# Loads and scaling of an output weight placed at marks within two steps of an attention loop

## The chip, the cores and the metric

The kernel runs on one core of a Trainium2 chip. The metric is device time in microseconds of the whole program, the median of three runs. A separate execution was recorded by the hardware profiler; every time from a "timeline" or a "group" comes from that execution and counts from the start of its span. The engines are PE (TensorE), DVE (VectorE), ACT (ScalarE), POOL (GpSimd) and SP (SyncE, which only issues transfers). Each takes its own instructions in its own order, and instructions of different engines wait for each other by semaphores.

## What is computed

One block of a transformer with modulated layer norms, in float32, 2048 tokens of width 512:

```python
mod = (silu(c) @ wmod).reshape(1, 6, 1, -1)
sa, ca, ga, sb, cb, gb = (mod[:, i] for i in range(6))
ga = (2 * (ga >= 0) - 1) * maximum(abs(ga), 0.25)      # gb likewise
h = layernorm(x) * (1 + ca) + sa
x = x + ga * attention(h, Q_w, ..., O_w, O_b)          # 16 heads of 128, causal
h = layernorm(x) * (1 + cb) + sb
x = x + gb * moe(h)                                    # 64 experts, top 4, and 2 shared ones
```

`attention` ends in a product of the heads' results with O_w (16 x 128 x 512). The kernel multiplies O_w by the gate ga once, so that the product is already gated.

## The kernel before

**Attention.** A loop runs over 80 steps: 16 heads, five steps each (`steps`, `BATCHES`). A step covers one or two pairs of query tiles of 128 rows: pair 7 in step 0, 6 in step 1, 5 and 0, 4 and 1, 3 and 2 in the others. For step n the loop emits, mixed with each other:
- the scores and exponentials of step n+2 (`softmax_work`): PE matmul ps (L408), DVE maximum (L420, L421), ACT exponential (L427), and DVE's normalisation of a finished row tile (L386 to L397);
- for step n+1, the turning of its probabilities: SP moves 32-row blocks of p to pt in 16 transfers (`swap_blocks`, L451, issued at the end of step n-1), and DVE turns each half (L461);
- for step n, the product with the values (`weighted_values`): PE matmul po (L479), ACT's copy of a finished pair to a tile `at` (L488, two buffers), and POOL's store of it to the array `atd` in DRAM (L489);
- a list of fillers for PE. For the last head these are the late rows of the modulation (`late_mod`, L529) and the output product of the first four token tiles over heads 0 to 14 (`begin_output`, L563), one tile in each of steps 1 to 4.

**What sets the order.** `merge` writes out the order by hand. It takes streams of (cost in PE columns, function), always emits from the stream that is furthest behind, and calls each function of `marks` once the given share of the step's whole cost has been emitted. The framework keeps this order on each engine and adds the semaphores. Marks at 0.55 and 0.8 turn the two halves of step n+1.

**The last head before the change.** At the head of its step 0 (L625 to L640) the kernel makes ga from its row (`gate`, DVE L105 to L110), issues from POOL's queue four transfers of 256 KB for the modulation row of cb (L521, `load_mod(4)`), then four of 1 MB that load O_w into the tile `wo` (L631; the profile calls it hT, whose memory it takes over), four of 256 KB for gb (`load_mod(5)`), and then multiplies the 16 heads of `wo` by ga, one POOL instruction of 128 x 512 for each (L636). Only then come, in POOL's order, the stores of the last head's pairs.

Readers of `wo` are `begin_output` (tile t=0, heads 0 to 14, in step 1) and, after the attention loop, the output phase (L899, L915). DRAM's `atd` of head 15 is read near the end of the loop (L658, L659) and in the output phase.

**After attention** come the output product, the second norm, routing, the experts with the shared experts in the gaps, and the gathering of the results. The change does not touch them.

Of the kernel before, what the change touches and what calls it, by code (L numbers as in the profile page):

```python
# [23 lines left out]
def adaln_block_kernel(  # L24
# [23 lines left out]
    nc = tc.nc  # L48
    _, N, D = x.shape
    H, _, DH = Q_w.shape  # L50
# [24 lines left out]
    ga = const.tile([P, D], F32)  # L75
# [48 lines left out]
    with ExitStack() as att:  # L124
# [57 lines left out]
        def make_q(hd, j):  # L182
            qts[hd, j] = project(0, j, hd, qtp, "qt")
# [4 lines left out]
        with tc.tile_pool(name="pre", bufs=1) as pre, tc.manual_schedule():  # L188
# [4 lines left out]
            for b in range(NB):  # L193
                xb = pre.tile([P, 4, D], F32, name="xb", bufs=NB)
                nc.sync.dma_start(
                    out=xb, in_=x[0, b * 512 : (b + 1) * 512, :].rearrange("(i p) d -> p i d", p=P)
                )
                xs.append(xb)
                if b == 0:
                    wms = {}  # L200
                    for i in (1, 0):
                        wms[i] = pre.tile([P, DC, D], F32, name="wm", bufs=2)
                        nc.sync.dma_start(
                            out=wms[i],
                            in_=wmod[:, i * D : (i + 1) * D].rearrange("(k p) n -> p k n", p=P),
# [116 lines left out]
        def make_v(g, t):  # L322

            if t == 0:
                vts[g] = vp.tile([P, NT, HG * DH], F32, name="v")
            wv, vb = groups[g]
            ps = psA.tile([P, HG * DH], F32, name="pv", tag="mm")
            for k in range(DC):
                nc.tensor.matmul(  # L329
                    out=ps,  # L330
                    lhsT=hT[:, k, t * P : (t + 1) * P],
                    rhs=wv[:, k].rearrange("p i d -> p (i d)"),
                    start=(k == 0),
                    stop=(k == DC - 1),
                )
            nc.vector.tensor_add(vts[g][:, t, :], ps, vb)
# [172 lines left out]
        def load_mod(i, queue):  # L509

            if i == 3:
                mods[i] = [ktp.tile([P, 512], F32, name="kt") for _ in range(DC)]
            elif i in (2, 4):
                both = [vow.tile([P, DC, HG, DH], F32, name="wv") for _ in range(2)]
                both = [w.rearrange("p k i d -> p (k i d)") for w in both]
                mods[i] = [both[k // 2][:, (k % 2) * D : (k % 2 + 1) * D] for k in range(DC)]
            else:
                four = [qkw.tile([P, DC, DH], F32, name=("wq", "wk")[k % 2]) for k in range(DC)]
                mods[i] = [w.rearrange("p k d -> p (k d)") for w in four]
            for k in range(DC):  # L520
                queue.dma_start(  # L521
                    out=mods[i][k], in_=wmod[k * P : (k + 1) * P, i * D : (i + 1) * D]
                )

        def late_mod(i, dst):

            pm = psA.tile([P, D], F32, name="pm", tag="mm")
            for k in range(DC):
                nc.tensor.matmul(  # L529
                    out=pm, lhsT=silc[:, k, :], rhs=mods[i][k], start=(k == 0), stop=(k == DC - 1)  # L530
                )
            if i == 4:
                nc.vector.tensor_scalar_add(dst, pm, 1.0)
            else:
                nc.vector.tensor_copy(dst, pm)
# [19 lines left out]
        def begin_output(t):  # L555
# [4 lines left out]
            def one(hd):  # L560
                if hd == 0:
                    box.append(psA.tile([P, D], F32, name="psb", tag="mm"))
                nc.tensor.matmul(  # L563
                    out=box[0],
                    lhsT=abs_[t // 2][:, hd, (t % 2) * P : (t % 2 + 1) * P],
                    rhs=wo[:, hd, :],
                    start=(hd == 0),
                    stop=(hd == H - 2),
                )
                if hd == H - 2:  # L570
                    if t == 0:
                        nc.vector.tensor_mul(rest[0][:, 1], rest[0][:, 0], ga)
                    nc.vector.tensor_add(parts[t], box[0], xts[t])
                    nc.vector.tensor_add(parts[t], parts[t], rest[0][:, 1])

            return [(512, lambda hd=hd: one(hd)) for hd in range(H - 1)]

        left = []

        def flush():  # L580
# [6 lines left out]
        def softmax_work(n):  # L587
            hd, s = steps[n]
            probs[n] = pp.tile([P, PW], F32, name="p")
            out = []  # L590
            for pr, i in tiles_of(s):
                out += softmax_tile(hd, s, pr, i, probs[n])
            return out

        def swap(n):
            flush()
            turned[n] = swap_blocks(steps[n][1], probs.pop(n))

        def turn(n, half):
            turn_blocks(steps[n][1], turned[n], half)  # L600

        with tc.manual_schedule():
            work = softmax_work(0) + softmax_work(1)
            fill = [(1024, lambda t=t: make_v(0, t)) for t in range(NT)]
            fill += [(2048, lambda j=j: make_q(0, j)) for j in (2, 0, 1)]
            merge([work[:4], fill[:8]], [])
            swap(0)
            merge([work[4:], fill[8:]], [])
            swap(1)
            turn(0, 0)  # L610
            turn(0, 1)
            for n, (hd, s) in enumerate(steps):
                if s == 3:
                    if hd + 2 < H:
                        heads[hd + 2] = load_head(hd + 2)
                    if hd % HG == 1 and hd // HG + 2 < NG:
                        groups[hd // HG + 2] = load_group(hd // HG + 2)
                fill = fillers(hd, s)
                if hd == H - 2 and s == 3:
                    load_mod(2, nc.sync)  # L620
                    load_mod(3, nc.sync)
                if hd == H - 2 and s == 4:
                    load_ab(0)
                    fill.append((2048, lambda: late_mod(2, ga)))
                if hd == H - 1 and s == 0:  # L625
                    mag = qkw.tile([P, DC, DH], F32, name="wq")
                    gate(mag.rearrange("p k d -> p (k d)"), ga)
                    load_mod(4, nc.gpsimd)
                    wo = hTp.tile([P, H, D], F32, name="hT")
                    for i in range(0, H, 4):  # L630
                        nc.gpsimd.dma_start(  # L631
                            out=wo[:, i : i + 4, :], in_=O_w[i : i + 4].rearrange("h p d -> p h d")
                        )
                    load_mod(5, nc.gpsimd)
                    for i in range(H):
                        nc.gpsimd.tensor_mul(wo[:, i, :], wo[:, i, :], ga)  # L636
                    fill += [
                        (2048, lambda i=i, dst=dst: late_mod(i, dst))
                        for i, dst in ((3, sb), (4, cb))
                    ]  # L640
                if hd == H - 1 and s == 1:
                    rest = [vow.tile([P, DC, HG, DH], F32, name="wv") for _ in range(2)]
                    rest = [w.rearrange("p (j k) i d -> p j (k i d)", j=2) for w in rest]
                    nc.sync.dma_start(out=rest[0][:, 0], in_=O_b.partition_broadcast(P))
                    for t in range(NE):
                        load_x_tile(t)
                    fill.append((2048, lambda: late_mod(5, gb)))
                if hd == H - 1 and s == 2:
                    gate(rest[1][:, 0], gb)
                if hd == H - 1 and s >= 1:  # L650
                    if s == 2:
                        place = pp.tile([P, PW], F32, name="p")[:, : (H - 1) * 2 * P]
                        load_ab(1, place.rearrange("p (h t) -> p h t", t=2 * P))
                    if s == 3:
                        load_ab(2)
                    if s == 4:
                        nc.vector.tensor_copy(ga, rest[0][:, 1])
                        nc.sync.dma_start(out=last3, in_=atd[H - 1, :, : (NE - 1) * P])  # L658
                        nc.sync.dma_start(out=ones, in_=atd[H - 1, :, (NE - 1) * P : NE * P])  # L659
                    fill += begin_output(s - 1)  # L660
                streams = [weighted_values(hd, s, turned.pop(n)), fill]
                if n + 2 < len(steps):
                    streams.insert(0, softmax_work(n + 2))
                marks = []
                if n + 1 < len(steps):
                    marks.append((0.55, lambda: turn(n + 1, 0)))
                    marks.append((0.8, lambda: turn(n + 1, 1)))
                merge([st for st in streams if st], marks)
                if n + 2 < len(steps):
                    swap(n + 2)  # L670
# [216 lines left out]
    with tc.manual_schedule():  # L887
# [9 lines left out]
        for t in range(NE):  # L897
            ps = psO.tile([P, D], F32, name="pso", tag="y")
            nc.tensor.matmul(  # L899
                out=ps,  # L900
# [8 lines left out]
        for t in range(NE, NT):  # L909
            pr, i = divmod(t, 2)  # L910
# [3 lines left out]
            for hd in range(H):  # L914
                nc.tensor.matmul(  # L915
                    out=ps,
# [281 lines left out]
```

## Time and profile before

| what | value |
|---|---|
| median of 3 runs | 2533.73 us |
| lowest and highest run | 2530.65 and 2536.56 us |
| profiled execution, its own time | 2545.0 us |
| span of the profile | 2543.2 us |
| mean granted TensorE clock | 0.989 |
| four 1 MB loads of O_w on POOL (L631) | 756 ns each to issue |
| sixteen scales of O_w on POOL (L636) | 1306 ns each, 20.3 us in all |
| 128 stores of head results on POOL (L489) | 613 ns each to issue |

The last three rows are from the groups of instructions by line. A POOL or SP row of a transfer is the time to issue it; the data lands later. In a timeline a row gives start, duration, engine, line, operation, tiles (written <- read), their count, and in brackets the idle time of the engine before it with what ended that.

The stage in question as windows of the span (busy us of each engine, granted clock, share of the DMA engines that was busy):

```profile
1653.60:1680.70 27.10, 14.53 (x51) 8.91 (x49) 17.04 (x30) 4.64 (x12) 18.33 (x21) 0.89 0.98 273
1680.70:1690.30 9.60, 9.58 (x21) 4.90 (x22) 7.51 (x9) 1.97 (x6) 9.60 (x9) 0.79 0.41 128
1690.30:1697.40 7.10, 7.10 (x22) 4.00 (x22) 2.67 (x9) 1.53 (x5) 0.55 (x2) 1.00 0.75 186
1697.40:1724.40 27.00, 27.00 (x81) 14.70 (x79) 17.00 (x32) 2.89 (x8) 0.55 (x1) 1.00 0.47 119
```

The columns after the window are its length, then PE, PE's weight loads, DVE, ACT and POOL (instructions in brackets), the clock, the DMA share, and GB/s.

### The profile page before, as it was taken

How to read it: one execution, taken by the hardware profiler on the slowest of the kernel's cores; microseconds unless marked ns; L12 is line 12 of the kernel's file. 1: busy time of each engine (PE TensorE's matmuls, PEld its weight loads, DVE VectorE, ACT ScalarE, POOL GpSimd, SP SyncE). 2: the span in 40 equal slices, each digit the busy share in tenths (PEclk: the TensorE clock that was granted, in tenths of full speed). 3: DMA queues.
4: the chain of work that ended last, by engine and by line, in shares of the span. 5: the costliest groups of instructions: out<-in, count | busy, mean ns of one | idle time of the engine just before them, and what ended most of it. 6: DMA issues, size and time to landing. Idle time of an engine off the chain costs nothing.

```text
span 2543.2 us, 25501 instructions
## 1 busy us (share of the span) xinstructions
PE 2445.4 (96%) x8297; PEld 1484.3 (58%) x8297; DVE 1431.6 (56%) x2737; ACT 647.1 (25%) x1456; POOL 247.3 (10%) x306
## 2 busy tenths in 40 slices
PE   7999999999999999999999999989999999999989
PEld 4666666666666666666666666545444456566534
DVE  4566666666666666666666666663655522222354
ACT  3233323333232333323333333311111121211100
POOL 0000000000000000000000000040000211111163
PEclk9999999999999999999999999999999999999989
DMA  4234434444444343444444434564521467767564
GB/s 137 60 98 97 115 90 108 112 101 111 98 121 107 93 118 99 96 119 101 109 118 101 109 97 97 161 188 135 203 83 50 124 190 229 226 201 233 168 187 138
DMA packets 225420, 326.21 MB, mean 128 GB/s; under 512 B 32100, under 2 KB 140680, under 8 KB 225288
## 3 DMA queue, kind: packets, MB, share of 16 engines
q1 hardware_dynamic: 197960, 251.16, 38.2%
q0 software_dynamic: 18112, 56.64, 7.0%
q10 hardware_dynamic: 9216, 16.78, 1.7%
q8 instruction: 67, 1.10, 0.2%
q14 instruction: 65, 0.53, 0.1%
HBM read 139.91 MB, written 41.94 MB: 72 GB/s over the span
## 4 chain that ended last, share of the span: by engine, by line
PE 65%; DVE 18%; SPq 6%; issue 4%; DMA 4%; ACT 2%; another core or an unknown queue 1%; DVEq 0%; ACTq 0%; POOL 0%; POOLq 0%
PE pqk L169 12%; PE ps L408 12%; PE po L479 9%; PE psg L973 8%; DVE pt L461 6%; SPq L451 6%; PE pv L329 5%; PE pso L915 4%; PE pse L1064 4%; PE psd L991 4%; DVE nm L421 4%; DMA pt<-p 3%; DVE p L397 3%; PE psy L1083 2%; PE tpx L1057 1%
## 5 line engine op out<-in xcount | busy, mean ns | idle before, releaser
L427 ACT ACTIVATE p<-ps,nm 128x1024 f32<-128x1024 f32 (+7 forms) x384 | 332.2, 865 | 1041.4 <-DVE nm L425 368.5
L408 PE MATMUL ps<-kt,qt 128*128 128x512 f32 (+3 forms) x1280 | 536.6, 536 | 44.5 <-ACT p L427 43.6
L479 PE MATMUL po<-pt,v 128*128 128x256 f32 (+1 forms) x2304 | 568.2, 369 | 6.6 <-DVE pt L461 3.6
L479 PEld LDWEIGHTS po<-pt,v 128*128 128x128 f32 x2304 | 426.2, 191 | 221.7 <-issue 156.5
L421 DVE TENSOR_REDUCE nm<-ps 128x1 f32<-128x1024 f32 (+7 forms) x384 | 349.6, 910 | 92.2 <-PE ps L408 83.4
L461 DVE STREAM_TRANSPOSE pt<-pt 128x1664 f32<-128x1664 f32 (+2 forms) x160 | 318.0, 1988 | 66.3 <-DMA pt<-p 61.5
L408 PEld LDWEIGHTS ps<-kt,qt 128*128 128x128 f32 x1280 | 235.4, 191 | 195.4 <-issue 127.4
L420 DVE TENSOR_TENSOR ps<-ps,causal 128x128 f32<-128x128 f32 x256 | 74.5, 291 | 349.9 <-PE ps L408 349.9
L329 PE MATMUL pv<-wv,hT 128*128 128x256 f32 x1024 | 240.3, 379 | 0.0
L489 POOL DMA_DIRECT2D atd<-at x128 | 78.4, 613 | 1652.2 <-ACT at L488 1627.7
L169 PE MATMUL pqk<-hT,wq 128*128 128x512 f32 x512 | 231.5, 595 | 0.0
L169 PE MATMUL pqk<-hT,wk 128*128 128x512 f32 x512 | 231.2, 595 | 0.0
L397 DVE TENSOR_SCALAR p<-p,rs 128x1024 f32<-128x1024 f32 (+7 forms) x384 | 221.8, 606 | 9.3 <-DMA p<-atd 0.2
L329 PEld LDWEIGHTS pv<-wv,hT 128*128 128x128 f32 x1024 | 194.5, 190 | 31.4 <-issue 1.9
L915 PE MATMUL pso<-hT,v 128*128 128x512 f32 x384 | 175.5, 604 | 0.0
L169 PEld LDWEIGHTS pqk<-hT,wk 128*128 128x128 f32 x512 | 98.0, 192 | 102.3 <-issue 99.7
L169 PEld LDWEIGHTS pqk<-hT,wq 128*128 128x128 f32 x512 | 97.9, 191 | 97.3 <-issue 94.2
L973 PE MATMUL psg<-h2T,wsu 128*128 128x512 f32 x256 | 119.2, 610 | 10.4 <-DVE sig L963 10.4
L1064 PE MATMUL pse<-wgu,xbT 128*128 128x256 f32 x512 | 121.1, 379 | 0.0
L973 PE MATMUL psg<-h2T,wsg 128*128 128x512 f32 x256 | 116.2, 593 | 4.8 <-ACT h2T L750 2.8
L915 PEld LDWEIGHTS pso<-hT,v 128*128 128x128 f32 x384 | 70.7, 192 | 74.5 <-issue 73.7
L991 PE MATMUL psd<-wsd,hs 128*128 128x512 f32 x256 | 111.5, 592 | 0.0
(224 smaller groups left out, 1723.0 us busy)
## 6 DMA issues: line engine op xcount, KB each, us to landing
pt<-p SPq DMA_DIRECT2D x768, 104.0 KB
pt<-p SPq DMA_DIRECT2D x256, 124.0 KB
pt<-p SPq DMA_DIRECT2D x256, 108.0 KB
atd<-at POOLq DMA_DIRECT2D x128, 128.0 KB
wgu<-in_L_ffn_Wg_dram SPq DMA_DIRECT2D x64, 256.0 KB
wgu<-in_L_ffn_Wu_dram SPq DMA_DIRECT2D x64, 256.0 KB
wd<-in_L_ffn_Wd_dram SPq DMA_DIRECT2D x64, 256.0 KB
ybd<-y ACTq DMA_DIRECT2D x64, 256.0 KB
```

Source lines behind the costliest of these rows:

```text
L169: nc.tensor.matmul(out=ps, lhsT=w[:, k, :], rhs=hT[:, k, j * 512 : (j + 1) * 512], start=(k == 0), stop=(k == DC - 1),)
L329: nc.tensor.matmul(out=ps, lhsT=hT[:, k, t * P : (t + 1) * P], rhs=wv[:, k].rearrange("p i d -> p (i d)"), start=(k == 0), stop=(k == DC - 1),
L397: nc.vector.tensor_scalar(cols[:, :, a:b], cols[:, :, a:b], rs[:, n : n + 1], None, ALU.mult)
L408: nc.tensor.matmul(out=ps[:, o : o + wo], lhsT=q, rhs=kts[hd, (c0 + o) // 512][:, :wo], start=True, stop=True,)
L421: nc.vector.tensor_reduce(nm[:, n : n + 1], ps[:, :w], AX.X, ALU.max, negate=True)
L427: nc.scalar.activation(rows[:, r0 + c0 // P : r0 + (c0 + w) // P], ps[:, :w].rearrange("q (r b k) -> q r b k", b=4, k=32), AF.Exp, bias=nm ...
L461: nc.vector.transpose(part, part)
L479: nc.tensor.matmul(out=po if wide else po[:, P:], lhsT=vts[g][:, kt, hh * DH : (hh + 1) * DH], rhs=rows[:, r : r + last + 1 : last] if wid ...
L915: nc.tensor.matmul(out=ps, lhsT=abs_[pr][:, hd, i * P : (i + 1) * P], rhs=wo[:, hd, :], start=(hd == 0), stop=(hd == H - 1),)
L973: nc.tensor.matmul(out=ps, lhsT=w[:, s, k, f * P : (f + 1) * P], rhs=h2T[:, k, b * 512 : (b + 1) * 512], start=(k == 0), stop=(k == DC - 1),)
L991: nc.tensor.matmul(out=ps, lhsT=hsh[b, f][:, i * P : (i + 1) * P], rhs=wsd[:, f, :], start=(f == 0), stop=(f == NHC - 1),)
L1064: nc.tensor.matmul(out=ps, lhsT=xts[e][:, k, :], rhs=weights[e][0][:, k].rearrange("p i h -> p (i h)"), start=(k == 0), stop=(k == DC - 1),)
```

## The change

The four loads of `wo`, the loads for gb and the 16 scales leave the head of step 0. They become functions that are called from marks in steps 0 and 1 of the last head: the loads at 0.05, 0.25, 0.4 and 0.55 of step 0, the loads for gb at 0.7, the scales of heads 0 to 3 in two pairs at 0.75 and 0.9 of step 0, and those of heads 4 to 15 in six pairs at 0.02 to 0.67 of step 1. The instructions are the same in kind and number, on the same engine.

```diff
+        def load_wo(i):
+            nc.gpsimd.dma_start(
+                out=wo[:, i : i + 4, :], in_=O_w[i : i + 4].rearrange("h p d -> p h d")
+            )
+
+        def scale_wo(i):
+            for j in (i, i + 1):
+                nc.gpsimd.tensor_mul(wo[:, j, :], wo[:, j, :], ga)
...
+        WO_LOADS = [(0.05, 0), (0.25, 4), (0.4, 8), (0.55, 12)]
+        WO_SCALES = [[(0.75, 0), (0.9, 2)], [(0.02, 4), (0.15, 6), (0.28, 8), (0.41, 10), (0.54, 12), (0.67, 14)]]
...
                     wo = hTp.tile([P, H, D], F32, name="hT")
-                    for i in range(0, H, 4):
-                        nc.gpsimd.dma_start(
-                            out=wo[:, i : i + 4, :], in_=O_w[i : i + 4].rearrange("h p d -> p h d")
-                        )
-                    load_mod(5, nc.gpsimd)
-                    for i in range(H):
-                        nc.gpsimd.tensor_mul(wo[:, i, :], wo[:, i, :], ga)
...
                 marks = []
+                if hd == H - 1 and s == 0:
+                    marks += [(f, lambda i=i: load_wo(i)) for f, i in WO_LOADS]
+                    marks.append((0.7, lambda: load_mod(5, nc.gpsimd)))
+                    marks += [(f, lambda i=i: scale_wo(i)) for f, i in WO_SCALES[0]]
+                if hd == H - 1 and s == 1:
+                    marks += [(f, lambda i=i: scale_wo(i)) for f, i in WO_SCALES[1]]
```

## The prediction, made before the result was seen

> **What bounds the kernel now.** I read the page first: busy time of the engines and the chain that ended last. The first line below gives busy time and share of the span for each engine, the second the shares of the last chain.
>
> ```profile
> PE 2445.4 (96%) x8297; PEld 1484.3 (58%) x8297; DVE 1431.6 (56%) x2737; ACT 647.1 (25%) x1456; POOL 247.3 (10%) x306
> PE 65%; DVE 18%; SPq 6%; issue 4%; DMA 4%; ACT 2%; another core or an unknown queue 1%; DVEq 0%; ACTq 0%; POOL 0%; POOLq 0%
> ```
>
> TensorE is the bound over the whole span, and POOL, the only engine whose work is edited, has 0% of the chain. So the question is one stage: steps 0 and 1 of head 15, about 1653 to 1724 us. I read POOL's timeline there next (start, duration, engine, line, operation, count, and in brackets the idle time before and what ended it).
>
> ```profile
> 1656.10 3.00 POOL L631 DMA_DIRECT2D hT<-in_L_attn_O_w_dram  x4
> 1662.95 0.54 POOL L521 DMA_DIRECT2D wk<-in_L_wmod_dram  x1 [1.14 <-DMA wv<-in_L_wmod_dram]
> 1669.05 4.99 POOL L636 TENSOR_TENSOR hT<-hT,ga 128x512 f32<-128x512 f32 x4 [5.56 <-DMA hT<-in_L_attn_O_w_dram]
> 1675.02 15.31 POOL L636 TENSOR_TENSOR hT<-hT,ga 128x512 f32<-128x512 f32 x12 [0.99 <-DMA hT<-in_L_attn_O_w_dram]
> 1690.26 0.59 POOL L489 DMA_DIRECT2D atd<-at  x1
> 1711.42 0.55 POOL L489 DMA_DIRECT2D atd<-at  x1 [20.57 <-ACT at L488]
> ```
>
> The four loads of wo are issued in 3.0 us, the 16 scales take 20.3 us, and the first store of head 15 stands behind them: it goes out at 1690.26, though its data was ready far earlier, as the first line of the next fence (ScalarE's timeline) shows: 1681.10 + 0.36 = 1681.46. The rest is PE's timeline. Each matmul stands there as two records, so "x4" of psb is two heads.
>
> ```profile
> 1681.10 0.36 ACT L488 COPY at<-po 128x256 f32<-128x256 f32 x1
> ...
> 1672.84 0.49 PE L408 MATMUL ps<-kt,qt 128*128 128x128 f32 x2 [3.62 <-ACT p L427]
> 1680.72 3.78 PE L408 MATMUL ps<-kt,qt 128*128 128x512 f32 x4 [7.17 <-ACT p L427]
> 1695.28 1.02 PE L563 MATMUL psb<-hT,v 128*128 128x512 f32 x2
> 1708.61 1.88 PE L563 MATMUL psb<-hT,v 128*128 128x512 f32 x4
> ```
>
> PE loses 3.62 and 7.17 us in this stage: 10.8 us. In the chain in order of time these lead back to "DMA pt<-p", 9.35 and 8.51 us long, where the same pieces elsewhere in that view take 2.3: the block swap of step 1 (SP's 16 transfers, issued from 1654.0) travels while 6 MB of weights, issued by POOL from 1653.6, land. The granted DMA share from 1653.6 to 1680.7 was 0.98. From 1680.72 to 1724.4 PE has no gap at all.
>
> **The loads.** In the source they move from the head of step 0 to the marks 0.05, 0.25, 0.4, 0.55, and the modulation load of gb to 0.7. But a mark is a place in the program's order, not a time: it delays nothing on POOL unless POOL meets, ahead of it, an instruction that waits. I therefore laid the two built programs' instructions side by side, engine by engine, with the semaphore values they wait for. PE, DVE, ACT and SP: the same rows in the same order, with the same waits. POOL: four loads for sb/cb, four of wo, four for gb, then scales, as before, because no store falls between these marks. So the loads go out at 1656.1 again, the 10.8 us of stalls stay, and this part costs 0.0 us and gains 0.0.
>
> **The one thing that moves.** The scales of heads 0 to 3 come before the store of step 0 and those of 4 to 15 behind it, where before all 16 stood ahead. No other store comes between the twelve: step 1's only store (1711.42) is emitted at the end of its stream. From the rows:
> - The store, before: 1690.26. After: POOL ends four scales at 1674.04, waits for ACT's copy until 1681.46, issues the store at 1681.5, 8.8 us earlier. Nobody gains: the tile's buffer is next wanted by the copy two stores later (ACT's copy at 1736.8), the stored columns are read only in the output phase, and the next store's wait is 20.57 us for ACT. Price 0.0 either way. Its 128 KB leave the stretch of step 2's swap, which starts at 1686.86; at that stage's 128 GB/s that is about 1 us of traffic (estimate), in front of a turn that waited for nothing. 0.0.
> - The wait that the change adds: POOL idles 1674.0 to 1681.5, with twelve scales queued behind the store. Who waits for them is PE: psb (L563) of head h needs scale h. The scales then run from 1682.05 at 1.276 us each (15.31/12). Scale 4 ends at 1683.3, psb of head 4 is at 1695.28: slack 12.0 us. Scale 14 ends at 1696.1, psb of head 14 is the second of the pair at 1708.61, so about 1709.5: slack 13.4. Head 15 is used after 1775. The slack cannot shrink by a shift of the stage, for the copy that releases the store and the scores that restart PE at 1680.72 come out of the same run of ScalarE's exponentials (1680.00 to 1681.46). Cover: 10 us of PE work between 1684.5 and 1695.3. If it were gone, the wait would cost up to the 7 us by which the scales are late. I take 0.0.
> - VectorE beside the scales. The next fence is DVE's timeline; the last two lines are the normal cost of two of these operations, from the groups by shape between 1000 and 1640 us (busy, mean ns).
>
> ```profile
> 1681.42 0.99 DVE L393 TENSOR_TENSOR rs<-rs,fix 128x1 f32<-128x1 f32 x1
> 1682.45 3.06 DVE L397 TENSOR_SCALAR p<-p,rs 128x1024 f32<-128x1024 f32 x2
> 1685.62 1.10 DVE L397 TENSOR_SCALAR p<-p,rs 128x128 f32<-128x128 f32 x1
> ...
> 1697.98 1.90 DVE L461 STREAM_TRANSPOSE pt<-pt 128x1664 f32<-128x1664 f32 x1
> 1700.63 1.23 DVE L421 TENSOR_REDUCE nm<-ps 128x1 f32<-128x1024 f32 x1 [0.74 <-PE ps L408]
> 1707.73 0.30 DVE L420 TENSOR_TENSOR ps<-ps,causal 128x128 f32<-128x128 f32 x1 [3.46 <-PE ps L408]
> ...
> L397 DVE TENSOR_SCALAR p<-p,rs 128x1024 f32<-128x1024 f32 x63 | 46.8, 753 | 2.0
> L393 DVE TENSOR_TENSOR rs<-rs,fix 128x1 f32<-128x1 f32 x50 | 8.0, 159 | 1.7
> ```
>
> Between scales, L393 took 0.99 for 0.16 and the pair (1024 and 384 wide) 3.06 for 0.75 + 0.42; the 128-wide one 1.10 for 0.28. Excess 0.83 + 1.89 + 0.82 = 3.5 us, about 0.9 each. After the change POOL is waiting or issuing the store until some 1682.1, so L393 and the 1024-wide one should be short and the two others long: some 1.8 us saved, at most 3.5. In return the scales now last until 1697.4 and meet the normalisation at 1696.4 to 1698.0 (L389, L393, two L397), which ran free: at most four times 0.9, 3.6 us, probably 1.8. Neither is on the path. The saving ends at 1686.6, where PE is in 43 us of continuous work; the loss is taken up by DVE's own idle time of 0.74 and 3.46 us, which ends with PE's scores at 1707.7. Bounds if the path took it all: -3.5 and +3.6 us; I take 0.0, since PE's unbroken run stands over both.
>
> Here the Trainium skill speaks against the change. "SBUF — State Buffer", section "Who interferes with whom", says that GpSimd's port pair is shared with VectorE under an exclusive lock: whoever issues first keeps it for the whole instruction, and the other stops. The rows agree in kind: an excess of 0.9 us is less than one scale of 1.28. By the rule the worst sum is a full scale per meeting, four meetings at 1.28: 5.1 us on DVE, where the rows give 3.6. Also by the rule VectorE may hold up POOL: bounded by the longest scale of this trace, 1.72 us, twelve scales end 5.3 us later than I have them, within the slack of 13. By either, the path sees 0.0.
>
> **Sum.** The profiled execution took 2545.0 us (span 2543.2): 2545.0 + 0.0 = 2545.0. It lies 11.3 us above the median of the three runs, so I carry the difference over, not the sum: 2533.7.
>
> **Rivals.** *It does what its words say*: the loads reach the queue one after another, the swap of step 1 is no longer behind 6 MB, and the two waits shrink from 9 us to the 2.3 of other swaps. PE gets its 10.8 us back: 2523. For it: the stalls are real and this is where they come from. Against it: POOL's queue has nothing in it that waits between those loads. 3 in 100.
> *Slower: the scales are late for PE.* Place: the twelve scales behind the store, before psb of heads 4 to 14. Head 14 decides first: it is on time while a scale takes less than (1709.5 - 1682.1)/11 = 2.5 us. If VectorE doubled each, to 3.1, PE would wait 6.6 us: 2540.3. For it: the port is visibly shared, and POOL's store at 1652.59 took 1.00 beside a normalisation instead of 0.54. Against it: one scale in sixteen reached 1.72, and DVE has few such operations between 1682 and 1697. 3 in 100.
> *VectorE's meetings reach the path*: at most +3.6 us, 2537.3, still within what cannot be told apart. It is in the main case's range.
>
> **How the numbers follow.** About 0.2%, 5 us, is what a measurement of this kernel can tell from no change; the three runs lie 5.9 us apart. Nothing measurable: 88 in 100, with the scatter of medians in it. Faster by more: 7, the first rival and scatter of medians. Slower: 5, the second and scatter. The range takes the DVE bounds, -3.5 and +3.6 us, with 1 us of scatter on each side: 2529.0 to 2538.5.
>
> **What would show it.** After: loads still at about 1656; POOL's groups show four scales, an idle stretch of some 7 us ended by ACT's copy, the store at about 1681.5, twelve scales to about 1697.5; PE's waits of 3.6 and 7.2 us still there; L393 short at 1681 and long at 1697; psb without a wait for POOL. I am wrong if the loads are found spread between 1656 and 1675, if PE waits for "POOL hT", or if the gap at 1724.5 (2.29 us, another swap) grows.

## The result: 0.37% slower, where no change was forecast

The changed kernel took 2541.19 us in the median of six runs (2539.88 to 2543.93), the kernel before 2531.32 us in six (2530.65 to 2536.56). The ratio is 1.0037, 95% interval 1.0024 to 1.0049: slower by 9.9 us, outside the range of 2529.0 to 2538.5.

The two spans say the opposite, and must not be compared: 2538.3 us after, 2543.2 before. Behind head 15's seventh store, where the change touches nothing, the profiled execution of before took 775.5 us (2543.2 - 1767.74) and that of after 763.4 (2538.3 - 1774.86). Most of the 12 us were lost near the end, while the results are gathered. Two windows show it, of before first and of after second (length, PE, PE's weight loads, DVE, ACT and POOL busy, clock, DMA share, GB/s): PE is busy 37.6 us of 50 in the one and 46.8 in the other.

```profile
2450.00:2500.00 50.00, 37.56 (x81) 16.08 (x80) 31.18 (x44) 2.88 (x5) 33.04 (x31) 0.86 0.66 204
```

```profile
2450.00:2500.00 50.00, 46.78 (x109) 20.36 (x108) 35.23 (x51) 3.58 (x6) 39.03 (x37) 1.00 0.79 236
```

So the stage itself is measured, from the last store of head 14 to the seventh store of head 15, both in POOL's timeline: 1652.59 to 1767.74 before, 115.15 us; 1649.76 to 1774.86 after, 125.10 us. The stage is 9.95 us longer, as much as the difference of the medians. Each length is that of one execution, and these scatter by some us (below, the stage of six_behind is 118.91 us long, and its median is that of before), so that the close agreement is in part luck.

POOL's timeline of the changed kernel shows what was forecast. The loads go out in one piece again, 3.1 us after head 14's last store (3.5 before); POOL stands idle 9.58 us for ACT; the store leaves at 1679.00, and the twelve scales begin 0.03 us behind it.

```profile
1649.76 1.00 POOL L489 DMA_DIRECT2D atd<-at  x1 [4.61 <-DMA v<-atd]
1652.87 2.98 POOL L526 DMA_DIRECT2D hT<-in_L_attn_O_w_dram  x4
1664.46 4.96 POOL L532 TENSOR_TENSOR hT<-hT,ga 128x512 f32<-128x512 f32 x4 [4.45 <-DMA hT<-in_L_attn_O_w_dram]
1679.00 0.64 POOL L489 DMA_DIRECT2D atd<-at  x1 [9.58 <-ACT at L488]
1679.67 14.71 POOL L532 TENSOR_TENSOR hT<-hT,ga 128x512 f32<-128x512 f32 x12
1716.86 0.59 POOL L489 DMA_DIRECT2D atd<-at  x1 [22.48 <-ACT at L488]
```

VectorE's timeline of the changed kernel has the loss (its rows are merged; the second line is the second half of the third, from the same timeline cut at 1679.2):

```profile
1678.58 0.16 DVE L393 TENSOR_TENSOR rs<-rs,fix 128x1 f32<-128x1 f32 x1
1679.44 15.16 DVE L397 TENSOR_SCALAR p<-p,rs 128x384 f32<-128x384 f32 x1
1678.77 15.83 DVE L397 TENSOR_SCALAR p<-p,rs 128x1024 f32<-128x1024 f32 x2
1694.70 0.29 DVE L397 TENSOR_SCALAR p<-p,rs 128x128 f32<-128x128 f32 x1
```

The 384-wide normalisation, 0.42 us elsewhere and 1.42 between the scales of before, took 15.16 us. It ended at 1694.60; the last scale ended at 1694.38. ScalarE waits behind it (the next exponential comes after 17.50 us), and PE, which still had scores and products to do, runs dry at 1691.6. PE's timeline of the changed kernel:

```profile
1670.30 0.49 PE L408 MATMUL ps<-kt,qt 128*128 128x128 f32 x2 [2.06 <-ACT p L427]
1677.96 3.78 PE L408 MATMUL ps<-kt,qt 128*128 128x512 f32 x4 [6.95 <-ACT p L427]
1691.05 0.59 PE L479 MATMUL po<-pt,v 128*128 128x256 f32 x2
1697.46 2.07 PE L408 MATMUL ps<-kt,qt 128*128 128x512 f32 x2 [5.82 <-ACT p L427]
1699.33 1.91 PE L572 MATMUL psb<-hT,v 128*128 128x512 f32 x2
```

The 5.82 us are a new wait. The rest is slower matmuls. The windows from PE's restart to the seventh store, of before and then of after:

```profile
1680.72:1767.74 87.02, 84.72 (x252) 47.40 (x253) 43.15 (x70) 12.20 (x32) 12.84 (x14) 0.98 0.51 141
```

```profile
1677.96:1774.86 96.90, 88.80 (x252) 49.01 (x253) 54.17 (x70) 12.20 (x32) 18.10 (x19) 0.93 0.45 123
```

PE's idle time grows from 2.30 to 8.10 us, and its busy time for the same 252 matmuls by 4.08 us, at a granted clock of 0.93 instead of 0.98: 5.8 + 4.1 = 9.9 us. The 4.1 us have two places. Right behind the new wait four lines (1697.46 to 1703.0) take 2.07, 1.91, 1.06 and 1.14 us, and the same ones in before 1.02, 1.02, 0.59 and 1.02: 2.5 us. Another 1.8 us (0.2 are gained elsewhere) stand behind a pause that before has too; PE's timeline of before and then of after:

```profile
1726.75 1.77 PE L408 MATMUL ps<-kt,qt 128*128 128x512 f32 x4 [2.29 <-ACT p L427]
```

```profile
1732.18 2.74 PE L408 MATMUL ps<-kt,qt 128*128 128x512 f32 x4 [2.27 <-ACT p L427]
```

That this second part comes from the change is not shown: in six_behind and no_gap_memsets, two of the experiments below that add no PE wait, the same line takes 3.35 us.

### The profile page after: what moved, and what is told of

It is laid out like the page before. It is cut to its first block, busy times and chain, and to the rows that moved or that the text cites. A ratio compares the mean times of both kernels' runs of the same rounds, so it can differ in the third digit from the quotient of the medians.

```text
span 2538.3 us, 25501 instructions
## 1 busy us (share of the span) xinstructions
PE 2445.8 (96%) x8297; PEld 1484.8 (58%) x8297; DVE 1441.7 (57%) x2737; ACT 647.3 (26%) x1456; POOL 247.2 (10%) x306
## 4 chain that ended last, share of the span: by engine, by line
PE 63%; DVE 18%; SPq 6%; issue 5%; DMA 4%; ACT 2%; POOL 1%; DVEq 0%; ACTq 0%; POOLq 0%
PE pqk L169 12%; PE ps L408 11%; PE po L479 9%; PE psg L987 7%; DVE pt L461 7%; SPq L451 6%; PE pv L329 5%; PE pso L929 4%; PE pse L1078 4%; PE psd L1005 4%; DVE nm L421 4%; DMA pt<-p 3%; DVE p L397 3%; PE psy L1097 2%; PE tpx L1071 1%
## 5 line engine op out<-in xcount | busy, mean ns | idle before, releaser
L397 DVE TENSOR_SCALAR p<-p,rs 128x1024 f32<-128x1024 f32 (+7 forms) x384 | 232.9, 635 | 9.3 <-DMA p<-atd 0.2
```

Source lines behind the costliest of these rows:

```text
L397: nc.vector.tensor_scalar(cols[:, :, a:b], cols[:, :, a:b], rs[:, n : n + 1], None, ALU.mult)
```

## The experiments

Theory S at the start: one VectorE operation on the port that it shares with POOL stands waiting as the run of scales begins, and is kept out until the whole run ends. (A run is a row of scales on POOL without idle time between them; a hold is the time for which a VectorE operation that meets the run stands still.) Rivals: P, the store's earlier place costs the time; M, each meeting costs 0.9 us as predicted and the loss is elsewhere. The experiments end P and M and change S; what is left of it stands in the last section. Ratios are to the kernel before, on the same chip. The last column is the whole duration of the longest VectorE operation that met a run of scales.

| run | median us | ratio (95%) | longest operation, us |
|---|---|---|---|
| store_on_act | 2531.27 | 0.9999 (0.9993 to 1.0006) | 1.7 |
| six_behind | 2530.51 | 0.9994 (0.9988 to 1.0001) | 7.81 |
| sixteen_behind | 2544.08 | 1.0045 (1.0032 to 1.0058) | 20.02 |
| pause_behind_store | 2529.88 | 0.9998 (0.9991 to 1.0004) | 1.3 |
| one_memset_behind | 2549.86 | 1.0020 (1.0013 to 1.0028) | 14.78 |
| broken_run | 2550.88 | 1.0025 (1.0016 to 1.0034) | 15.61 |
| no_store_on_pool | 2542.78 | 0.9992 (0.9984 to 1.0000) | 1.32 |
| loads_behind_swap | 2528.91 | 0.9939 (0.9926 to 0.9953) | 1.7 |
| no_store_early_run | 2529.52 | 0.9994 (0.9986 to 1.0003) | 1.18 |
| load_inside_run | 2532.05 | 1.0002 (0.9994 to 1.0010) | 1.7 |
| normalise_on_act | 2532.19 | 1.0001 (0.9993 to 1.0009) | 5.73 |
| load_right_ahead | 2541.98 | 1.0042 (1.0026 to 1.0059) | 9.62 |
| no_gap_memsets | 2530.43 | 0.9993 (0.9984 to 1.0002) | 1.7 |
| gap_memsets | 2530.68 | 0.9993 (0.9983 to 1.0004) | 1.7 |

one_memset_behind, broken_run, no_store_on_pool and loads_behind_swap ran on a chip where the kernel before took 2544.07 us; of these four only the ratios and the differences among them count.

### store_on_act: the store leaves POOL's queue

```diff
+                        queue = nc.scalar if (hd, s) == (H - 1, 0) else nc.gpsimd
-                        nc.gpsimd.dma_start(out=atd[hd, :, pr * 256 : (pr + 1) * 256], in_=at)
+                        queue.dma_start(out=atd[hd, :, pr * 256 : (pr + 1) * 256], in_=at)
```

> The changed kernel with one difference: the first store of the last head leaves from ScalarE's queue instead of POOL's, so that the 16 scales run without a break from about 1664 us and nothing in POOL's queue waits for ACT. Theory S (one VectorE normalisation, caught as the run of twelve scales begins behind the store, is kept out until the run ends): the 384-wide L397 falls from 15.2 us to under 2, PE's new wait of 5.8 us is gone, time about 2531 (the kernel before), within 3 us. Rival P (what costs is that the store itself goes out earlier): the store is early here too, so the time stays at about 2541. Rival M (each meeting costs 0.9 us, the loss is elsewhere): 2541 as well.

The loss is gone. The store is early here too (issued at 1679.83, from ScalarE's queue), so P falls; VectorE's operations take the 0.99, 1.72, 1.42 and 1.10 us that they took before.

### six_behind and sixteen_behind: the dose

```diff
-        WO_SCALES = [[(0.75, 0), (0.9, 2)], [(0.02, 4), (0.15, 6), (0.28, 8), (0.41, 10), (0.54, 12), (0.67, 14)]]
+        WO_SCALES = [[(0.75, 0), (0.8, 2), (0.85, 4), (0.9, 6), (0.95, 8)], [(0.41, 10), (0.54, 12), (0.67, 14)]]
```

and, for sixteen behind, the first list empty and all eight pairs in the second.

> The changed kernel with ten scales ahead of the first store and six behind it, instead of four and twelve. Theory S: the 384-wide L397 is held for the whole run of six, 6 x 1.226 + 0.4 = 7.8 us instead of 15.2; VectorE is free some 9.7 us after PE's restart instead of 17.0, PE does not run dry (it did after 13.1 us), time 2531 to 2534. Rival P: 2541, the store's place is unchanged. Rival M: the normalisation pair takes some 3 us, time as in the changed kernel, 2541.

> The changed kernel with all sixteen scales behind the first store. Theory S: the 384-wide L397 is held for 16 x 1.226 + 0.4 = 20.1 us, 4.9 more than with twelve, and since PE has run dry by then all of it lands on the path: 2541 + 4.9 = 2546. Rival P: 2541. Rival M: 2541, or a little more if psb has to wait for its scales.

The groups by shape of VectorE (busy, mean ns, idle before), of six_behind and then of sixteen_behind:

```profile
L397 DVE TENSOR_SCALAR p<-p,rs 128x384 f32<-128x384 f32 x1 | 7.8, 7809 | 0.0
```

```profile
L397 DVE TENSOR_SCALAR p<-p,rs 128x384 f32<-128x384 f32 x1 | 20.0, 20023 | 0.0
```

Six, twelve and sixteen scales hold it for 7.81, 15.16 and 20.02 us: 1.22 us for each further scale, which is the distance from scale to scale, and 0.45 once. With six, PE does not run dry and the time is that of before, though the hold is there: the loss is not the hold but what of it PE cannot cover. (In its one profile the stage is 3.8 us longer than in before, 2.6 of it PE's slower matmuls; the medians of 21 and 59 executions don't show this.) With sixteen PE waits 10.54 us instead of 5.82, 4.7 more. The median rose by 2.9 us over the changed kernel's, less than the 4.9 expected, and the two intervals overlap; the trace, not the time, carries the dose. M falls.

### pause_behind_store and one_memset_behind: when the run begins

```diff
                 if hd == H - 1 and s == 1:
+                    for _ in range(6):
+                        nc.gpsimd.memset(pad, 0.0)
                     marks += [(f, lambda i=i: scale_wo(i)) for f, i in WO_SCALES[1]]
```

(`pad` is an unused tile of 128 x 96; one memset instead of six in the second run.)

> The changed kernel with six small memsets of an unused 128 x 96 tile on POOL between the store and the twelve scales (about 1.2 us), so that the scales begin after the 384-wide L397 should have ended. Theory S, with the phase deciding (an operation that stands waiting when the run begins loses the whole run; one that comes into a run already going loses at most one scale): the pair takes about 1.2 us, at most 3, and the time is about 2531. If any operation that meets a run behind a store loses the whole run whatever the phase: the next one, 128 wide, takes 14 us instead, 2541. Rival P: 2541.

> The changed kernel with one memset instead of six behind the store, so that the run of twelve begins some 0.3 us later than in the changed kernel: after the 384-wide L397 has ended, and about when the 128-wide one begins. Theory S with the phase deciding: if the first scale begins inside the 128-wide operation, that one is held for the whole run (12 x 1.226 + 0.3, about 15 us) and the time is about 2541; if it begins before or after it, the hold is at most one scale and the time about 2531. In no case is the 384-wide one held. If instead the store's transfer is what makes the hold, nothing is held behind a memset: 2531 whatever the phase.

With six the run begins 1.47 us behind the store's issue and nothing is held for more than a scale, not even the operations that meet it 13 us later (L390 0.77, L394 0.99 us). With one it begins 0.29 us behind, and the 128-wide operation is caught. POOL's and then VectorE's timeline of one_memset_behind:

```profile
1679.92 0.65 POOL L490 DMA_DIRECT2D atd<-at  x1 [8.71 <-ACT at L489]
1680.56 0.33 POOL L679 MEMSET pad<- 128x96 f32 x1
1680.86 1.26 POOL L533 TENSOR_TENSOR hT<-hT,ga 128x512 f32<-128x512 f32 x1
```

```profile
1680.88 14.78 DVE L398 TENSOR_SCALAR p<-p,rs 128x128 f32<-128x128 f32 x1
```

The stage (head 14's last store to head 15's seventh) is 125.2 us long, as in the changed kernel. Its ratio, 1.0020 (5.8 us), is little more than half of that. Against no_store_on_pool, on the same chip and without a long hold, its median is 7.1 us longer and its stage 9.5 (125.2 and 115.7). All four kernels on this chip look better against before by their medians than by their stages, by 2 to 7 us; no profile of before was taken there, and why is open.

### broken_run: a memset after each scale

```diff
                 nc.gpsimd.tensor_mul(wo[:, j, :], wo[:, j, :], ga)
+                if i >= 4:
+                    nc.gpsimd.memset(pad[:, 6 * j : 6 * j + 6], 0.0)
```

> The changed kernel with a memset of 128 x 6 after each of the twelve scales (0.1 us each, none waits for anything). It asks whether an instruction that only writes lets VectorE in. If it does: the 384-wide L397 is held for one scale, at most 2 us, time about 2531. If the run counts as unbroken: held for 12 x 1.33 + 0.4, about 16.4 us, time about 2542.

Held for 15.61 us, to the end of the run: an instruction that only writes, with no idle time around it, did not let VectorE in. The loss, 0.25%, is smaller than the 0.4% expected, as it is in one_memset_behind on this chip.

### no_store_on_pool and no_store_early_run: no transfer ahead of the run

```diff
+                        final = (hd, s) == (H - 1, 0)
+                        queue = nc.scalar if final else nc.gpsimd
+                        if final:
+                            nc.scalar.copy(pad, at[:, :96])
+                            for _ in range(2):
+                                nc.gpsimd.memset(pad, 0.0)
-                        nc.gpsimd.dma_start(out=atd[hd, :, pr * 256 : (pr + 1) * 256], in_=at)
+                        queue.dma_start(out=atd[hd, :, pr * 256 : (pr + 1) * 256], in_=at)
```

(one memset in the second run)

> The changed kernel with the first store of the last head on ScalarE's queue; in its place POOL runs two memsets, the first of which waits for a small copy that ScalarE makes behind its copy of the head's result. So the twelve scales again begin behind a wait for ACT, at about the phase of the changed kernel, but no transfer is issued on POOL. Theory S with the phase deciding: if the first scale begins inside the 384-wide or the 128-wide L397, that one is held for the whole run, about 15 us, and the time is about 2541. If the issue of a transfer on POOL is what makes the hold: no hold, about 2531.

> As no_store_on_pool, with one memset instead of two, so that the twelve scales begin about 0.2 us after the start of the 384-wide L397, as in the changed kernel, and again with no transfer issued by POOL. If the phase alone decides: the 384-wide one is held for the whole run, about 15 us, time 0.4% above the kernel before. If it takes the issue of a transfer right ahead of the run: held for one scale, about 1.3 us, time as before within 0.1%.

Here the theory's "phase" falls. POOL's and then VectorE's timeline of no_store_on_pool: the 128-wide operation starts 0.02 us after the first scale, exactly as in one_memset_behind, and is held for one scale instead of twelve.

```profile
1682.10 1.26 POOL L539 TENSOR_TENSOR hT<-hT,ga 128x512 f32<-128x512 f32 x1
```

```profile
1682.12 1.32 DVE L398 TENSOR_SCALAR p<-p,rs 128x128 f32<-128x128 f32 x1
```

In no_store_early_run the scales begin 0.16 us after the 384-wide operation's start (0.23 in the changed kernel); it ends in 0.41 us, and the first scale takes 1.37 us: POOL waits, not VectorE. What separates the pairs is the transfer that POOL issues ahead of the run. In these two runs the same store leaves from ScalarE's queue, 0.86 and 0.52 us ahead of the scales. A transfer of another queue that comes closer does not make the hold either: SP issued one that ended 0.08 us before the run of loads_behind_swap and 0.19 us before that of pause_behind_store, and VectorE came in after at most one scale.

### load_inside_run and load_right_ahead: another transfer, in the order of before

One of the four transfers for gb is issued between scales 3 and 4 of the kernel before, then between scales 5 and 6:

```diff
                     for i in range(H):
+                        if i == 4:
+                            one_mod(5, DC - 1, nc.gpsimd)
                         nc.gpsimd.tensor_mul(wo[:, i, :], wo[:, i, :], ga)
```

> The kernel before (16 scales ahead of the first store) with the last of the four transfers for gb issued from POOL between scale 3 and scale 4, some 5 us before VectorE's first normalisation meets the run. If a transfer ahead of a run shuts VectorE out until the run ends, whenever it comes: L393 or the 1024-wide L397 is held from about 1680 to the end of the run at about 1690, some 8 us instead of 1. If the operation has to be standing at the run's start: 1 to 2 us for each, as before, and the time within 0.1% of the kernel before.

> As load_inside_run, with the transfer between scales 5 and 6, where the next scale waits for no data, so that a run of ten begins right behind it, as behind the store in the changed kernel. VectorE's normalisation meets the run some 5 us after its start. If a transfer right ahead of a run shuts VectorE out until the run ends, whenever it comes: L393 or the 1024-wide L397 is held until the run ends, some 6 us instead of 1. If the operation has to be standing there as the run begins: 1 to 2 us for each, as in the kernel before. The time is within 0.1% of the kernel before in both cases, because PE has some 5 us in hand there.

In the first, scale 4 waited for its data and began 0.82 us behind the transfer: nothing is held longer than in before. In the second, a run of ten begins right behind it. POOL's, VectorE's and PE's timeline of load_right_ahead:

```profile
1676.29 0.58 POOL L524 DMA_DIRECT2D wk<-in_L_wmod_dram  x1
1676.88 12.24 POOL L641 TENSOR_TENSOR hT<-hT,ga 128x512 f32<-128x512 f32 x10
```

```profile
1678.63 0.27 DVE L420 TENSOR_TENSOR ps<-ps,causal 128x128 f32<-128x128 f32 x1
1678.93 0.56 DVE L421 TENSOR_REDUCE nm<-ps 128x1 f32<-128x384 f32 x1
1679.52 9.62 DVE L425 TENSOR_TENSOR nm<-nm 128x1 f32<-128x1 f32 x1
```

```profile
1689.90 3.78 PE L408 MATMUL ps<-kt,qt 128*128 128x512 f32 x4 [16.48 <-ACT p L427]
```

This reproduces the loss without the change: no store is moved, no scale waits for ACT, and the operation caught is another one, 2.6 us into the run, a minimum of two columns of 128 x 1 that takes 0.16 us elsewhere. It was held to the end of the run at 1689.12. So it need not stand there as the run begins. The two operations before it, which take an operand from PSUM, pass freely. My expectation for the time was wrong: L425 lies ahead of the exponential that PE waits for, so PE's wait grew from 7.2 to 16.5 us.

### no_gap_memsets and gap_memsets: what ends the state

Both have sixteen scales behind the store, with eight memsets that wait for nothing, or two of which the second waits for the first, in between:

```diff
+                    for j in range(8):
+                        nc.gpsimd.memset(pad[:, 12 * j : 12 * j + 12], 0.0)
```

> The changed kernel with all sixteen scales behind the first store and, between store and scales, eight memsets of 128 x 12 in columns of their own, which wait for nothing and so leave no gap (about 0.6 to 1 us). VectorE's three L397 at 1679 should be done before the run of scales; the next operation that needs the port is L389 near 1694, and the run ends near 1700. If only a gap in POOL's stream ends the state: L389 (or L425 before it) is held till about 1700, 5 us or more. If the time passed ends it: under 1.3 us each. Time: 0.1 to 0.5% above the kernel before in the first case, within 0.1% in the second.

> The same with two memsets in the same columns, of which the second waits for the first (gap about 0.06 us, some 0.4 us in all). If a gap ends the state: no operation held for more than 1.3 us, time within 0.1% of the kernel before. If it is time that must pass: held to the end of the run, 20 us for an L397 near 1679 or 5 us for L389 near 1694, time 0.1 to 0.5% above.

POOL's and then VectorE's timeline of no_gap_memsets:

```profile
1677.01 0.65 POOL L490 DMA_DIRECT2D atd<-at  x1 [19.83 <-ACT at L489]
1677.64 0.42 POOL L680 MEMSET pad<- 128x12 f32 x8
1678.01 20.13 POOL L533 TENSOR_TENSOR hT<-hT,ga 128x512 f32<-128x512 f32 x16
```

```profile
1677.97 1.41 DVE L398 TENSOR_SCALAR p<-p,rs 128x128 f32<-128x128 f32 x1
```

In neither kernel is anything held for longer than a scale, at the run's start or later. The scales begin 0.36 and 0.38 us behind the store's issue. In the first there is no gap between store and scales, so an idle gap is not needed to end the state; with 0.29 us and one memset it was still on. Whether the passed time decides or the number of instructions in between is open, and so is what happens inside POOL.

### normalise_on_act: the caught operation moved away

```diff
+                    if (hd, s) == (H - 1, 2):
+                        nc.scalar.activation(
+                            cols[:, :, a:b], cols[:, :, a:b], AF.Identity, scale=rs[:, n : n + 1]
+                        )
+                        continue
```

> The changed kernel with the normalisation of step 2's probabilities of the last head (the L397 that is caught) on ScalarE instead of VectorE; POOL's order is the changed one. Theory S: nothing on VectorE stands at the port when the run begins, PE's wait of 5.8 us is gone and the time is that of the kernel before, within 0.1%. If the loss came from the place of the store or of the scales: 0.4% above the kernel before, as the changed kernel.

The order on POOL is the changed one, and the time is that of before: with the caught operation gone, so is the loss. But the hold is not. POOL's scales run from 1680.87 to 1695.59, right behind the store, and the next operation that needs the port meets them 9.0 us later. VectorE's and then PE's timeline of normalise_on_act:

```profile
1689.87 5.73 DVE L430 TENSOR_TENSOR nm<-nm 128x1 f32<-128x1 f32 x1
```

```profile
1696.26 1.98 PE L413 MATMUL ps<-kt,qt 128*128 128x512 f32 x4 [0.77 <-ACT p L432]
```

It was held to the run's end, like the one in load_right_ahead; PE had enough to do and lost 0.77 us.

### loads_behind_swap: what the change's words say, done

```diff
-                    for i in range(0, H, 4):
-                        nc.gpsimd.dma_start(
+                    load_mod(5, nc.sync)
+                    for i in range(0, H, 4):
+                        nc.sync.dma_start(
                             out=wo[:, i : i + 4, :], in_=O_w[i : i + 4].rearrange("h p d -> p h d")
                         )
-                    load_mod(5, nc.gpsimd)
```

> The kernel before (scales in one row, ahead of the store) with the row for gb and the four loads of O_w moved from POOL's to SP's queue, where they stand behind the 16 transfers of step 1's swap. Does what the change's words say. The swap then shares the engines with 1 MB instead of 6: PE's waits of 3.6 and 7.2 us should shrink by up to 8 us. Against that, the swap of step 2 now stands behind 5 MB on SP's queue, and may be 4 us late for its turn. Expected 2523 to 2530; 2531 or more if the wait only moves to the next swap.

On SP's queue the loads stand behind the swap's 16 transfers, and that holds them back. PE's and POOL's timeline of loads_behind_swap:

```profile
1670.81 3.63 PE L408 MATMUL ps<-kt,qt 128*128 128x512 f32 x4 [2.74 <-ACT p L427]
```

```profile
1674.46 20.16 POOL L636 TENSOR_TENSOR hT<-hT,ga 128x512 f32<-128x512 f32 x16 [20.71 <-DMA hT<-in_L_attn_O_w_dram]
```

The waits of 3.62 and 7.17 us have become one of 2.74, and the stage takes 107.2 us instead of 115.15: 7.9 us, about the 8 expected. The wait that was feared for the next swap did not come: step 2's turn starts without one. The scales begin behind a wait for data, with no transfer of POOL's just ahead, and VectorE passes between them. This version beats the kernel before, and with it the changed one. Of its ratio of 0.9939 (15 us, where 1 to 8 were expected) the stage explains about half. The rest is not shown to come from the edit: behind the stage, where nothing was changed, its profiled execution took 769.7 us and that of no_store_on_pool, on the same chip, 775.8.

## Why the prediction was wrong, point by point

- *The loads*: right. Issued in one piece at the same place; PE's waits stayed (2.06 and 6.95 us). The first rival fell as argued, and loads_behind_swap shows that its stalls were real.
- *The store*: right. Out early, behind a wait for ACT; worth nothing by itself (store_on_act 0.9999).
- *The scales behind the store*: right. PE had its scales in time: the largest wait of psb for POOL in the trace is 0.2 us. The slower rival's mechanism did not happen. (Its sum had a slip: twice 1.28 is 2.6 us, not 3.1, and the wait would have been under 1 us, not 6.6.)
- *VectorE beside the scales*: this is the step that failed, in the price of 0.9 us for a meeting. The sum "some 1.8 us saved, at most 3.5" counted the 384-wide normalisation as one such meeting; it cost 14.7 us (15.16 for 0.42). The four meetings of the other sum, "at most four times 0.9, 3.6 us", did not take place: with everything late, L389 and L393 ran at 1700.5 to 1701.1, behind the scales, in 0.21 and 0.16 us. The 0.9 us were read from rows in which VectorE met a run that POOL had begun after idle time. The change put the issue of a transfer 0.03 us ahead of a run of twelve. The rows of before held no run behind a transfer, so the price of a meeting should not have been taken from them without an upper end: the whole run.
- *The cover*: also failed. "43 us of continuous work" on PE was not independent of VectorE; PE needs a new exponential within it and ran dry 13.7 us after its restart. The rival "VectorE's meetings reach the path" named the right mechanism, but priced it at 3.6 us at most instead of 9.9, and for the meetings at 1696 to 1698, not for the one that was caught.
- *The Trainium skill's rule* ("SBUF — State Buffer", "Who interferes with whom": the one that starts first keeps the port for the whole instruction) pointed the right way, and its sum of 5.1 us was nearer than mine. But by it a hold ends with one scale, 1.28 us; here it lasted six, twelve and sixteen scales. Nor did starting first help: the 384-wide normalisation began at 1679.44, 0.23 us before the first scale, and lost; in no_store_early_run it began 0.16 us before it, and POOL waited. Behind a transfer the measurement goes beyond the rule.

## What to carry to other kernels

A small edit in one queue can change nothing but what stands right ahead of what, and that can cost more than the work moved: look at which instruction a run on POOL now follows. When POOL and VectorE share operands in SBUF, give a meeting two prices, one instruction and the whole unbroken run, and ask what PE does if it is the second. A mark in the program's order holds nothing back; a place behind other transfers in the same queue does.

## What the runs showed of the hardware

A run of POOL multiplications begun within 0.3 us of the end of POOL's issue of a transfer kept one of VectorE's two-operand or scaling operations in SBUF out to the run's end (it took 5.73, 7.81, 9.62, 14.78, 15.16, 15.61, 20.02 us in seven kernels), whether the operation met it at its start or 9 us into it. Begun 0.36 us or more behind it, or without a transfer of POOL's, VectorE came in after at most one scale (nine kernels, where the longest operation took 1.2 to 1.7 us). VectorE's reductions and copies from PSUM and its block transposes passed in both states. What ends this state lies between 0.30 and 0.36 us or in the instructions in between; that is open. And right behind the new PE wait of 5.8 us four lines of matmuls took 2.5 us longer than in before.
